# Token choice of layer 0 in a written order, with the context products of layer 1 beside it

## The chip, the cores and the metric

The kernel runs on one core of one Trainium2 chip. The metric is the device time of one execution in microseconds; the time of a kernel is the median of three runs. A profile is one further execution, recorded by the hardware profiler.

## The reference

Two layers work on x of 2 x 2048 tokens with 512 features, and on a context of 2 x 154 tokens. All of it is float32.

```python
x = x + L0_xattn(layernorm(x), ctx)                  # 16 heads
x = x + L0_ffn(layernorm(x))                         # below
x = x + L1_xattn(layernorm(x), ctx, Wq, bq, Wk, bk, Wv, bv)   # one head of 512
x = x + L1_ffn(layernorm(x))                         # top 2 of 8 experts, and a shared one

def L0_ffn(x):                                       # E = 8 experts, K = 1024
    scores = softmax(xf @ router_w + router_b)
    G, idx = top_k(scores.T, K)                      # each expert takes its 1024 best tokens
    toks = xf[idx]
    h1 = relu(toks @ w1 + b1); eo = h1 @ w2 + b2
    y[idx] += eo * G
```

So in layer 0 each expert chooses tokens: of 4096 scores the 1024 highest, ties to the lower token number. This choice is what the change rewrites, together with the products of layer 1's context (K, V and their like), which depend on inputs alone.

## The kernel before, in words

The kernel has four stages, one after the other. Attention of layer 0 ends with the scores of all tokens in `scores` (128 partitions, 8 experts x 32 token tiles) and with each normalized token and its scores in DRAM, 32 stores `xs<-row` (L403). Then comes the choice (L494 to L670). Then the experts of layer 0 run as 16 blocks of 512 tokens, with their products in a Strassen-like form of seven products of half blocks. Then follow attention and experts of layer 1.

The choice works in this way. Two transposes (`pt_s`, L573) bring the scores into the form of 8 experts x 16 runs of 256 tokens, one run a partition, and L574 copies them to `sco`. A search by bits then finds each expert's threshold, in 30 steps. In a step, DVE compares all scores with the threshold and counts a run (`cmp`, `cnt`, L591); PE sums the 16 counts of an expert with a matrix of ones, `same`, (`pc`, L579); DVE turns the sum into the next bit (`off`, L594) and the next threshold (`thr`, L595). Each of these waits for the one before it. After the search, L612 to L634 mark the chosen tokens (`sel`, `eq`), number them with two scans and two products with `tri` (`run`, `before`), transpose the numbers back (`pt_p`, L627) and split them into `hi` and `lo`.

From these the list of an expert's tokens is made: `list_head` (`ohhi`, `val`, L728 to L735), four times `list_part` (`ohlo`, L740) with `list_sum` (32 small products `ps_list`, L752), and `list_end` (`idx`, L764). With `idx`, POOL gathers token tiles from `xs` (`xg`, L773); `turn` transposes them (L112, `xgT`), and DVE makes sums of them (`xsum`, L791 to L794). POOL makes sums of the weights w1 (`sw`, L817). The products of a block (`prod`, L709) take turns with these. The first seven are p1, p6, p2, p7, p5, p3, p4; p1 needs `xgT` alone, p6 the second of `xsum` and the second of `sw`.

The context products are: `ps_k` (4 times 4 matmuls of 308 columns, L643), copied by ACT to `kpT`; `ps_kw` (the same with Wq, L650) to `kw`; `ps_bqk` (4, L658) to `bqk`; and `ps_v` (4 times 4 matmuls of 512 columns, L665), to which DVE adds the bias (`vp`, L668). `kw` and `vp` go to DRAM (L669, L670) and come back in layer 1. The profile counts each float32 matmul as two, since PE passes it twice; "x4" in a line is thus two matmuls.

What sets the order: attention and the experts stand in `tc.manual_schedule`, where the order of the code is the order on PE, DVE, ACT and POOL. The choice and the context products stand outside of it; there a scheduler orders each engine's instructions. It puts nine of the search's `pc` first, and then the products of `ps_k`, `ps_kw` and `ps_bqk` between the later ones; most of `ps_v` stands after the search. DMA issues on SP are always in the scheduler's order: w1q, ctxT, wk, wqT, wv, bq, bk, bv_bc, three more w1q, four w2q, kw_d, vp_d.

Memory: pools are stacked. `const` lasts for the whole kernel. `wm` holds the quarters of w1 and w2 (tags `w1` and `w2`, four buffers of 8 KB a partition each). `sr` and the PSUM pool `pr` hold all of the choice and of the context products, and are closed ahead of the experts, whose pools `sm` and `pm` take the same memory. A tile in such memory waits until the older tile's users, its DMAs among them, are done.

Of the kernel before, what the change touches and what calls it, by code (L numbers as in the profile page):

```python
# [20 lines left out]
P = 128  # L21
# [13 lines left out]
E = 8  # L35
# [20 lines left out]
def two_layers(ctx: ExitStack, tc: tile.TileContext, a, out):  # L56
# [34 lines left out]
    io_p = const.tile([P, 1], F32, name="io_p")  # L91

# [404 lines left out]
    with tc.tile_pool(name="wm", bufs=4) as wm:  # L497
# [9 lines left out]

        with (
            tc.tile_pool(name="sr", bufs=1) as sr,
            tc.tile_pool(name="pr", bufs=1, space=PSUM) as pr,  # L510
        ):

            ctxT = sr.tile([P, KC, B * TKV], F32, name="ctxT")
            nc.sync.dma_start(ctxT, a["ctxT"].rearrange("(k p) n -> p k n", p=P))
            wk = sr.tile([P, KC, D], F32, name="wk1")
            wv = sr.tile([P, KC, D], F32, name="wv1")
            wqT = sr.tile([P, KC, D], F32, name="wqT1")
            for w, n in ((wk, "Wk"), (wqT, "WqT"), (wv, "Wv")):
                nc.sync.dma_start(w, a[n].rearrange("(k p) n -> p k n", p=P))
# [8 lines left out]
            for q in range(4):  # L528
                load_w2(0, q)

            def iota(dst, pattern, mult):
                i = sr.tile(dst.shape, I32, name="iota_i")
                nc.gpsimd.iota(i, pattern=pattern, base=0, channel_multiplier=mult)
                nc.vector.tensor_copy(dst, i)

            iota(io128, [[1, P]], 0)
            iota(io8, [[1, CAP // P]], 0)
            iota(io_t, [[1, NT]], 0)
            iota(io_p, [[1, 1]], 1)

            same = sr.tile([P, E, NR], F32, name="same")
            tri = sr.tile([P, E, NR], F32, name="tri")
            nc.gpsimd.affine_select(
                same,
                ones.rearrange("p (e r) -> p e r", e=E),
                pattern=[[-NR, E], [0, NR]],
                compare_op=ALU.is_ge,
                fill=0.0,  # L550
                base=0,
                channel_multiplier=1,
            )
            nc.gpsimd.affine_select(
                same,
                same,
                pattern=[[NR, E], [0, NR]],
                compare_op=ALU.is_ge,
                fill=0.0,
                base=NR - 1,  # L560
                channel_multiplier=-1,
            )
            nc.gpsimd.affine_select(
                tri, same, pattern=[[NR, E], [1, NR]], compare_op=ALU.is_gt, fill=0.0, base=0, channel_multiplier=-1
            )
            same = same.rearrange("p e r -> p (e r)")
            tri = tri.rearrange("p e r -> p (e r)")
            half = RUN // P
            sco = sr.tile([P, half, P], F32, name="sco")
# [4 lines left out]
            nc.vector.tensor_copy(sco, pt)  # L574
            sco = sco.rearrange("p h n -> p (h n)")

            def per_expert(v, m, name):
                ps = pr.tile([P, 1], F32, tag="pc", name=name)
                nc.tensor.matmul(ps, m, v, start=True, stop=True)  # L579
                return ps  # L580
# [3 lines left out]
            thr = sr.tile([P, 1], I32, name="thr")  # L584
            nc.vector.memset(thr, 1 << 29)
            off = sr.tile([P, 1], I32, name="off")
            cmp = sr.tile([P, RUN], F32, name="cmp")
            cnt = sr.tile([P, 1], F32, name="cnt")
# [16 lines left out]
            nc.vector.memset(zero, 0.0)  # L605
# [6 lines left out]
            nc.vector.tensor_scalar(sel, sco, thrf, None, ALU.is_gt, ALU.add, accum_out=cnt)  # L612
            nc.vector.tensor_scalar(eq, sco, thrf, None, ALU.is_equal)
            pc = per_expert(cnt, same, "pc")
# [20 lines left out]


            kw = sr.tile([P, KC, B * TKV], F32, name="kw")
            vp = sr.tile([KV2, B, 2, D], F32, name="vp")
            kpT = sr.tile([P, KC, B * TKV], F32, name="kpT")
            for c in range(KC):  # L640
                ps = pr.tile([P, D], F32, tag="pre", name="ps_k1", bufs=2)
                for k in range(KC):
                    nc.tensor.matmul(  # L643
                        ps[:, : B * TKV], wk[:, k, ts(c, P)], ctxT[:, k, :], start=k == 0, stop=k == KC - 1
                    )
                nc.scalar.activation(kpT[:, c, :], ps[:, : B * TKV], AF.Identity, bias=bk[:, c : c + 1])
            for c in range(KC):
                ps = pr.tile([P, D], F32, tag="pre", name="ps_kw", bufs=2)
                for k in range(KC):
                    nc.tensor.matmul(  # L650
                        ps[:, : B * TKV], wqT[:, k, ts(c, P)], kpT[:, k, :], start=k == 0, stop=k == KC - 1
                    )
                nc.scalar.mul(kw[:, c, :], ps[:, : B * TKV], -scale1)
            bq_bc = sr.tile([P, KC, P], F32, name="bq_bc")
            nc.gpsimd.tensor_copy(bq_bc, bq.unsqueeze(2).to_broadcast([P, KC, P]))
            ps = pr.tile([P, D], F32, tag="pre", name="ps_bqk", bufs=2)
            for k in range(KC):
                nc.tensor.matmul(ps[:, : B * TKV], bq_bc[:, k, :], kpT[:, k, :], start=k == 0, stop=k == KC - 1)  # L658
            nc.scalar.mul(bqk, ps[:, : B * TKV], -scale1)
            for b in range(B):  # L660
                for j in range(2):
                    ps = pr.tile([P, D], F32, tag="pre", name="ps_v1", bufs=2)
                    n0 = b * TKV + j * KV2
                    for k in range(KC):
                        nc.tensor.matmul(  # L665
                            ps[:KV2, :], ctxT[:, k, n0 : n0 + KV2], wv[:, k, :], start=k == 0, stop=k == KC - 1
                        )
                    nc.vector.tensor_tensor(vp[:, b, j, :], ps[:KV2, :], bv_bc[:KV2, :], ALU.add)  # L668
            nc.sync.dma_start(kw_d, kw)  # L669
            nc.sync.dma_start(vp_d, vp)  # L670
# [16 lines left out]
        with (  # L687
# [36 lines left out]
            def list_head(e):  # L724
                shape = [P, NT, CAP // P]
                ohhi = sm.tile(shape, BF16, tag="ohhi", name="ohhi", bufs=1)
                val = sm.tile([P, NT, 2, CAP // P], BF16, tag="val", name="val", bufs=1)
                nc.vector.tensor_tensor(  # L728
                    ohhi,
                    hi[:, e, :].unsqueeze(2).to_broadcast(shape),  # L730
                    io8.unsqueeze(1).to_broadcast(shape),
                    ALU.is_equal,
                )
                nc.vector.tensor_tensor(val[:, :, 0, :], ohhi, io_t.unsqueeze(2).to_broadcast(shape), ALU.mult)
                nc.vector.tensor_scalar_mul(val[:, :, 1, :], ohhi, io_p)  # L735
                lst[e] = (val, pm.tile([P, 2, CAP // P], F32, tag="tr", name="ps_list"))

            def list_part(e, q):
                oh = sm.tile([P, LG, P], BF16, tag="ohlo", name="ohlo")
                nc.vector.tensor_tensor(  # L740
                    oh,
                    lo[:, e, q : q + LG].unsqueeze(2).to_broadcast([P, LG, P]),
                    io128.unsqueeze(1).to_broadcast([P, LG, P]),
                    ALU.is_equal,
                )
                lst[e, q] = oh
# [13 lines left out]
            def list_end(e):  # L760
                _, ps = lst.pop(e)
                part = sm.tile([P, CAP // P], F32, tag="part", name="part")
                nc.vector.tensor_copy(part, ps[:, 1, :])
                nc.vector.scalar_tensor_tensor(idx[:, e, :], ps[:, 0, :], float(P), part, ALU.mult, ALU.add)  # L764
# [4 lines left out]
            def gather(b, t):  # L769
                e, half = divmod(b, CAP // TB)  # L770
                col = half * TPB + t
                xg[b, t] = sm.tile([P, ROW], F32, tag="xg", name="xg", bufs=4)
# [7 lines left out]
            def turn(b, t):  # L780
                e = b // (CAP // TB)
                if t == 0:
                    xT[b] = sm.tile([P, KC, TB], F32, tag="xT", name="xgT", bufs=1)
                g = xg.pop((b, t))
                gates[b, t] = sm.tile([P, 1], F32, tag="gate", name="gate", bufs=12)
                nc.vector.tensor_copy(gates[b, t], g[:, D + e : D + e + 1])
                transpose_tile(g[:, 0:D], xT[b], t, pm, "tr")
# [12 lines left out]
            def sum_x(b):  # L800
                xsum[b] = sm.tile([P, 3, 2, HB], F32, tag="xsum", name="xsum", bufs=1)
# [10 lines left out]
            def sum_w1(b, q, part):  # L812
                a11, a12, a21, a22 = blocks_of_w1(b // (CAP // TB), q)
                for i in (0, 1) if part == 0 else (2, 3):
                    o = s1w[b, q, i] = sm.tile([P, 2, 2, P], F32, tag="sw", name="sw", bufs=6)
# [163 lines left out]

            list_head(0)  # L980
# [6 lines left out]
            sum_w1(0, 0, 0)  # L987
            sum_w1(0, 0, 1)
            sum_w1(0, 1, 0)
# [702 lines left out]
```

## Time and profile before

| what | us |
|---|---|
| median of three runs | 3005.03 (3000.24 to 3007.15) |
| the profiled execution | 3016.07 |
| its span | 3014.4 |
| PE busy in the span | 2778.1 (92%) |
| DVE, ACT, POOL busy | 1547.0, 880.1, 1216.7 |
| last scores of layer 0 written | 627.6 |
| search: first comparison to `sel` | 634.22 to 681.62 |
| `lo` written, list begun (`ohhi`), `idx` written | 689.94, 703.58, 710.12 |
| first gather, first product of a block (p1), p6 | 711.18, 719.90, 723.71 |

Times inside the profile are counted from the span's start. A line of a timeline has start, length, engine, line of the code, operation, tiles (out<-in), shapes, how many; in brackets stands how long the engine had been idle and what ended that. PE is the array, PEld its weight loads, SPq what SP issues. The granted clock is the share of full speed that PE was given in the stretch. A table of stretches gives the engines' busy time in each.

### The profile page before, as it was taken

The page shows a single profiled execution, that of the slowest core. Times are in us where ns is not written, and L with a number is a line of the kernel's source. Part 1 is how long each engine was busy: PE and PEld are TensorE (multiplying, and loading weights), DVE is VectorE, ACT ScalarE, POOL GpSimd, SP SyncE. Part 2 cuts the span into 40 slices and gives each one's busy share as a digit, 9 for nine tenths or more (in the row PEclk, how much of TensorE's full clock was granted, in tenths as well). Part 3 has the DMA queues.
Part 4 walks back from the last instruction along what each step waited for, and adds up shares of the span by engine and source line. Part 5 has one row for each costly group of instructions (what it writes and reads, how often), then busy time and mean ns, then how long its engine had stood idle before and what let it go on. Part 6 is the DMA issues. An engine that isn't in the chain of part 4 may idle for free. (4 is left out here: it accounts for less than half of the span.)

```text
span 3014.4 us, 38792 instructions
## 1 busy us (share of the span) xinstructions
PE 2778.1 (92%) x14262; PEld 2133.2 (71%) x14262; DVE 1547.0 (51%) x2933; ACT 880.1 (29%) x1854; POOL 1216.7 (40%) x986
## 2 busy tenths in 40 slices
PE   7889998867999999999999999999995888889995
PEld 4444554445888888888888888888885655567773
DVE  4677776544545435444454355443532555544355
ACT  2555554411122112212122112211220555432331
POOL 1445544403344424343334333432431555465552
PEclk9899999878999999999999999999998999899998
DMA  4011111161122231231222312312113642143387
GB/s 160 18 36 46 47 61 47 53 219 38 25 77 84 44 111 25 78 86 27 67 81 70 88 22 78 88 29 85 56 15 80 220 81 64 47 92 129 133 315 282
DMA packets 127083, 256.47 MB, mean 85 GB/s; under 512 B 16508, under 2 KB 22668, under 8 KB 126742
## 3 DMA queue, kind: packets, MB, share of 16 engines
q1 hardware_dynamic: 93232, 170.79, 16.9%
q0 software_dynamic: 29056, 74.81, 10.8%
q10 hardware_dynamic: 4608, 8.39, 0.7%
q8 instruction: 115, 1.88, 0.3%
q14 instruction: 72, 0.59, 0.1%
HBM read 176.09 MB, written 77.85 MB: 84 GB/s over the span
## 5 line engine op out<-in xcount | busy, mean ns | idle before, releaser
L831 ACT ACTIVATE H<-H,b_sb 128x256 f32<-128x256 f32 (+1 forms) x384 | 198.9, 571 | 563.0 <-DVE H L882 287.0
L928 POOL TENSOR_TENSOR eo<-eo,b_bc 128x512 f32<-128x512 f32 x64 | 96.4, 1506 | 647.4 <-DVE eo L974 585.4
L709 PE MATMUL prod<-w2q,H 128*128 128x256 f32 x1536 | 346.9, 379 | 0.0
L709 PEld LDWEIGHTS prod<-w2q,H 128*128 128x128 f32 x1536 | 289.5, 190 | 38.1
L312 POOL TENSOR_TENSOR pr<-pr,sm 128x616 f32<-128x616 f32 x128 | 155.2, 1213 | 275.5 <-DVE sm L311 249.7
L709 PE MATMUL prod<-xsum,sw 128*128 128x256 f32 x1024 | 245.4, 380 | 0.7 <-DVE xsum L792 0.7
L709 PE MATMUL prod<-xgT,w1q 128*128 128x256 f32 x1024 | 243.2, 380 | 0.0
L709 PE MATMUL prod<-xgT,sw 128*128 128x256 f32 x1024 | 243.1, 380 | 0.0
L709 PE MATMUL prod<-tw,hs 128*128 128x256 f32 x1024 | 234.5, 380 | 0.0
L817 POOL TENSOR_TENSOR sw<-w1q 128x512 f32<-128x512 f32 x128 | 189.6, 1481 | 84.3 <-PE prod L709 84.0
L709 PEld LDWEIGHTS prod<-xgT,w1q 128*128 128x128 f32 x1024 | 195.5, 191 | 26.8
L709 PEld LDWEIGHTS prod<-tw,hs 128*128 128x128 f32 x1024 | 192.8, 190 | 27.8 <-PE prod L709 2.5
L709 PEld LDWEIGHTS prod<-xsum,sw 128*128 128x128 f32 x1024 | 193.3, 190 | 26.7 <-POOL sw L817 1.0
L709 PEld LDWEIGHTS prod<-xgT,sw 128*128 128x128 f32 x1024 | 193.4, 190 | 25.7
L113 ACT COPY xgT<-pt 128x512 f32<-128x512 f32 x64 | 37.5, 585 | 431.7 <-PE pt L112 431.7
L900 POOL DMA_INDIRECT xacc<-eo,idx x64 | 100.6, 1572 | 153.0 <-DMA xacc<-eo,idx 92.1
L1513 PE MATMUL ph<-xgT,wc 128*128 128x128 f32 x1248 | 152.6, 275 | 7.4 <-DVE wc L1503 6.0
L289 DVE TENSOR_REDUCE mx<-sc 128x4 f32<-128x616 f32 x128 | 101.8, 795 | 105.5 <-PE sc L285 103.5
L1513 PEld LDWEIGHTS ph<-xgT,wc 128*128 128x128 f32 x1248 | 145.6, 192 | 9.0 <-issue 5.3
L1528 PE MATMUL po<-wall,h1r 128*128 x312 | 146.7, 593 | 1.7 <-issue 1.7
L1536 DVE TENSOR_TENSOR y<-po,wall 128x512 f32<-128x512 f32 x78 | 53.9, 691 | 144.1 <-PE po L1528 134.1
L1485 POOL DMA_INDIRECT xg<-xn,xrow x78 | 84.1, 1079 | 106.6 <-PE pt L1120 100.6
(296 smaller groups left out, 5156.9 us busy)
## 6 DMA issues: line engine op xcount, KB each, us to landing
w1q<-in_w SPq DMA_DIRECT2D x32, 1024.0 KB
w2q<-in_w SPq DMA_DIRECT2D x32, 1024.0 KB
y<-ys SPq DMA_DIRECT2D x40, 256.0 KB
xs<-row SPq DMA_DIRECT2D x32, 260.0 KB
x_sb<-in_x SPq DMA_DIRECT2D x32, 256.0 KB
x<-in_x SPq DMA_DIRECT2D x32, 256.0 KB
xacc<-x SPq DMA_DIRECT2D x32, 256.0 KB
x<-xacc SPq DMA_DIRECT2D x32, 256.0 KB
```

Of the source, the lines that this page charges most:

```text
L113: nc.scalar.copy(dstT[:, :, ts(t, P)], pt)
L289: nc.vector.tensor_reduce(mx, sc[:, :, 0:TKV], AX.X, ALU.min)
L312: nc.gpsimd.tensor_tensor(pr, pr, sm.to_broadcast([P, 4, TKV]), ALU.mult)
L709: nc.tensor.matmul(ps[:, g, :], w, m, start=i == 0, stop=i == len(terms) - 1)
L817: nc.gpsimd.tensor_tensor(o, l, m, ALU.add if i == 0 else ALU.subtract)
L831: nc.scalar.activation(dst, src, AF.Relu, bias=b1_sb[:, e, f : f + 1])
L900: nc.gpsimd.indirect_dma_start(out=xacc[:, :], out_offset=bass.IndirectOffsetOnAxis(ap=idx[:, e, col : col + 1], axis=0), in_=eo, in_offse ...
L928: nc.gpsimd.tensor_tensor(eo, eo, b2_bc, ALU.add)
L1485: nc.gpsimd.indirect_dma_start(out=xg[r], out_offset=None, in_=G_.xn[:, :], in_offset=bass.IndirectOffsetOnAxis(ap=G_.xrow[:, i : i + 1], ...
L1513: nc.tensor.matmul(ph[:, c, :], wc[:, k * HE + c * P : k * HE + (c + 1) * P], x_[:, k, :], start=k == 0, stop=k == KC - 1,)
L1528: nc.tensor.matmul(po_[r], h[:, c, :], wflat[:, bass.ds(at + (W2_AT + c * D), D)], start=c == 0, stop=c == HE // P - 1)
L1536: nc.vector.tensor_tensor(y, po_.pop(r), wflat[:, bass.ds(at + B2_AT, D)], ALU.add)
```

## The change

The stage of choice and context products now also stands in `manual_schedule`. Its pieces:

- The iota constants, `same`, `tri` and the tiles of the search (`sco`, `cmp`, `cnt`, `off`, `thr`) move to `const`, and the constants are made at the kernel's start.
- The context products become a generator, `ctx_part`. After each `pc` or `before` product, `per_expert` lets it put out one piece: two matmuls of 308 columns, or one of 512. What is left follows after the last use of the search.
- Wk, WqT, ctxT and Wv are loaded into the four buffers with the tag `w2`, in this order, ahead of w1; the four quarters of w2 come when these are free. In the order that the built program has on SP: Wk, WqT, ctxT, Wv, bq, bk, bv_bc, four w1q, two w2q, kw_d, one w2q, vp_d, one w2q.
- The bias of `vp` is added by POOL, after a copy by ACT, and not by DVE. `zero` is set by POOL.
- The list's tiles, gathered rows, `xgT`, `xsum`, `sw` and `gate` move to a pool `sl` and a PSUM pool `pl` of their own, opened before `sr` and `pr`; `sm` and `pm` keep the rest.
- `sum_w1` of the first block stands ahead of the list in the code. In the built program its six additions stand on POOL ahead of the four additions for `vp`, and the four gathers come behind those.
- `pc` after the search stands ahead of `eq` in the code, and `room` so comes ahead of the first scan on DVE.

```diff
+    def iota(dst, pattern, mult, name):
+        i = const.tile(dst.shape, I32, name=name)
+        nc.gpsimd.iota(i, pattern=pattern, base=0, channel_multiplier=mult)
+        nc.vector.tensor_copy(dst, i)
...
+    sco = const.tile([P, RUN], F32, name="sco")
+    cmp = const.tile([P, RUN], F32, name="cmp")
+    cnt = const.tile([P, 1], F32, name="cnt")
+    off = const.tile([P, 1], I32, name="off")
+    thr = const.tile([P, 1], I32, name="thr")
+    nc.vector.memset(thr, 1 << 29)
...
+        def load_ctx(n, cols):
+            t = wm.tile([P, 4, D], F32, tag="w2", name=n + "1")[:, :, 0:cols]
+            nc.sync.dma_start(t, a[n].rearrange("(k p) n -> p k n", p=P))
+            return t
+
+        sl = outer0.enter_context(tc.tile_pool(name="sl", bufs=2))
+        pl_ = outer0.enter_context(tc.tile_pool(name="pl", bufs=2, space=PSUM))
         with (
             tc.tile_pool(name="sr", bufs=1) as sr,
             tc.tile_pool(name="pr", bufs=1, space=PSUM) as pr,
+            tc.manual_schedule(engines={ET.PE, ET.DVE, ET.Activation, ET.Pool}),
         ):
-            ctxT = sr.tile([P, KC, B * TKV], F32, name="ctxT")
-            nc.sync.dma_start(ctxT, a["ctxT"].rearrange("(k p) n -> p k n", p=P))
...
+            wk = load_ctx("Wk", D)
+            wqT = load_ctx("WqT", D)
+            ctxT = load_ctx("ctxT", B * TKV)
+            wv = load_ctx("Wv", D)
...
             for q in range(4):
                 load_w1(0, q)
-            for q in range(4):
-                load_w2(0, q)
...
+            def ctx_part():
+                def sums(w, m, n):
+                    ps = pr.tile([P, D], F32, tag="pre", name="ps_c", bufs=2)
+                    for k in range(KC):
+                        nc.tensor.matmul(ps[: w(k).shape[1], 0:n], w(k), m(k), start=k == 0, stop=k == KC - 1)
+                        if k < KC - 1 and (k % 2 or n == D):
+                            yield ps
+                    yield ps
+
+                for c in range(KC):
+                    for ps in sums(lambda k: wk[:, k, ts(c, P)], lambda k: ctxT[:, k, :], B * TKV):
+                        yield
+                    nc.scalar.activation(kpT[:, c, :], ps[:, : B * TKV], AF.Identity, bias=bk[:, c : c + 1])
...
+                        for ps in sums(lambda k: ctxT[:, k, n0 : n0 + KV2], lambda k: wv[:, k, :], D):
+                            yield
+                        nc.scalar.copy(vp[:, b, j, :], ps[:KV2, :])
+                        nc.gpsimd.tensor_tensor(vp[:, b, j, :], vp[:, b, j, :], bv_bc[:KV2, :], ALU.add)
+                nc.sync.dma_start(vp_d, vp)
+
+            beside = ctx_part()
...
             def per_expert(v, m, name):
                 ps = pr.tile([P, 1], F32, tag="pc", name=name)
                 nc.tensor.matmul(ps, m, v, start=True, stop=True)
+                next(beside, None)
                 return ps
...
-            nc.vector.memset(zero, 0.0)
+            nc.gpsimd.memset(zero, 0.0)
...
+            pc = per_expert(cnt, same, "pc")
             nc.vector.tensor_scalar(eq, sco, thrf, None, ALU.is_equal)
-            pc = per_expert(cnt, same, "pc")
...
-                    nc.vector.tensor_tensor(vp[:, b, j, :], ps[:KV2, :], bv_bc[:KV2, :], ALU.add)
-            nc.sync.dma_start(kw_d, kw)
-            nc.sync.dma_start(vp_d, vp)
+            for _ in beside:
+                pass
+            for q in range(4):
+                load_w2(0, q)
...
-                ohhi = sm.tile(shape, BF16, tag="ohhi", name="ohhi", bufs=1)
-                val = sm.tile([P, NT, 2, CAP // P], BF16, tag="val", name="val", bufs=1)
+                ohhi = sl.tile(shape, BF16, tag="ohhi", name="ohhi", bufs=1)
+                val = sl.tile([P, NT, 2, CAP // P], BF16, tag="val", name="val", bufs=1)
...
+            sum_w1(0, 0, 0)
+            sum_w1(0, 0, 1)
+            sum_w1(0, 1, 0)
             list_head(0)
...
             for t in range(TPB):
                 gather(0, t)
-            sum_w1(0, 0, 0)
-            sum_w1(0, 0, 1)
-            sum_w1(0, 1, 0)
```

More of the change, by code (lines that the diff above doesn't have):

```diff
@@ L91, in two_layers @@
     io_p = const.tile([P, 1], F32, name="io_p")
+    def iota(dst, pattern, mult, name):
+        i = const.tile(dst.shape, I32, name=name)
+        nc.gpsimd.iota(i, pattern=pattern, base=0, channel_multiplier=mult)
+        nc.vector.tensor_copy(dst, i)
+    iota(io128, [[1, P]], 0, "io128_i")
+    iota(io8, [[1, CAP // P]], 0, "io8_i")
+    iota(io_t, [[1, NT]], 0, "io_t_i")
+    iota(io_p, [[1, 1]], 1, "io_p_i")
+    same = const.tile([P, E, NR], F32, name="same")
+    tri = const.tile([P, E, NR], F32, name="tri")
+    nc.gpsimd.affine_select(
+        same,
+        ones.rearrange("p (e r) -> p e r", e=E),
+        pattern=[[-NR, E], [0, NR]],
+        compare_op=ALU.is_ge,
+        fill=0.0,
+        base=0,
+        channel_multiplier=1,
+    )
+    nc.gpsimd.affine_select(
+        same,
+        same,
+        pattern=[[NR, E], [0, NR]],
+        compare_op=ALU.is_ge,
+        fill=0.0,
+        base=NR - 1,
+        channel_multiplier=-1,
+    )
+    nc.gpsimd.affine_select(
+        tri, same, pattern=[[NR, E], [1, NR]], compare_op=ALU.is_gt, fill=0.0, base=0, channel_multiplier=-1
+    )
+    same = same.rearrange("p e r -> p (e r)")
+    tri = tri.rearrange("p e r -> p (e r)")
+    half = RUN // P
+    sco = const.tile([P, RUN], F32, name="sco")
[4 more added lines that the diff above has]
+    nc.vector.memset(thr, 1 << 29)
     def layernorm(src, dst, small):
@@ L496, in two_layers @@
     vp_d = dram.tile([KV2, B, 2, D], F32, name="vp_d")
-    with tc.tile_pool(name="wm", bufs=4) as wm:
+    with ExitStack() as outer0:
+        wm = outer0.enter_context(tc.tile_pool(name="wm", bufs=4))
         w1s, w2s = {}, {}
@@ L510, in two_layers @@
             tc.tile_pool(name="pr", bufs=1, space=PSUM) as pr,
+            tc.manual_schedule(engines={ET.PE, ET.DVE, ET.Activation, ET.Pool}),
         ):
-            ctxT = sr.tile([P, KC, B * TKV], F32, name="ctxT")
-            nc.sync.dma_start(ctxT, a["ctxT"].rearrange("(k p) n -> p k n", p=P))
[L515 to L519, printed above, removed]
+            wk = load_ctx("Wk", D)
+            wqT = load_ctx("WqT", D)
+            ctxT = load_ctx("ctxT", B * TKV)
+            wv = load_ctx("Wv", D)
             bq = sr.tile([P, KC], F32, name="bq")
@@ L527, in two_layers @@
                 load_w1(0, q)
-            for q in range(4):
-                load_w2(0, q)
[L531 to L569, printed above, removed]
+            kpT = sr.tile([P, KC, B * TKV], F32, name="kpT")
+            kw = sr.tile([P, KC, B * TKV], F32, name="kw")
+            vp = sr.tile([KV2, B, 2, D], F32, name="vp")
@@ new lines, in two_layers @@
+            bq_bc = sr.tile([P, KC, P], F32, name="bq_bc")
+            nc.gpsimd.tensor_copy(bq_bc, bq.unsqueeze(2).to_broadcast([P, KC, P]))
+            def ctx_part():
[10 more added lines that the diff above has]
+                    nc.scalar.activation(kpT[:, c, :], ps[:, : B * TKV], AF.Identity, bias=bk[:, c : c + 1])
+                for c in range(KC):
+                    for ps in sums(lambda k: wqT[:, k, ts(c, P)], lambda k: kpT[:, k, :], B * TKV):
+                        yield
+                    nc.scalar.mul(kw[:, c, :], ps[:, : B * TKV], -scale1)
+                for ps in sums(lambda k: bq_bc[:, k, :], lambda k: kpT[:, k, :], B * TKV):
+                    yield
+                nc.scalar.mul(bqk, ps[:, : B * TKV], -scale1)
+                nc.sync.dma_start(kw_d, kw)
+                for b in range(B):
+                    for j in range(2):
+                        n0 = b * TKV + j * KV2
+                        for ps in sums(lambda k: ctxT[:, k, n0 : n0 + KV2], lambda k: wv[:, k, :], D):
+                            yield
+                        nc.scalar.copy(vp[:, b, j, :], ps[:KV2, :])
+                        nc.gpsimd.tensor_tensor(vp[:, b, j, :], vp[:, b, j, :], bv_bc[:KV2, :], ALU.add)
+                nc.sync.dma_start(vp_d, vp)
@@ L573, in two_layers @@
                 nc.tensor.transpose(pt[:, i, :], by_run[:, i, :], ident)
-            nc.vector.tensor_copy(sco, pt)
-            sco = sco.rearrange("p h n -> p (h n)")
+            nc.vector.tensor_copy(sco.rearrange("p (h n) -> p h n", h=half), pt)
             def per_expert(v, m, name):
@@ L579, in per_expert @@
                 nc.tensor.matmul(ps, m, v, start=True, stop=True)
+                next(beside, None)
                 return ps
[L584 to L588, printed above, removed]
             thrf = thr.bitcast(F32)
@@ L634, in two_layers @@
             nc.vector.tensor_copy(lo, pos)
[L637 to L667, printed above, removed]
-                    nc.vector.tensor_tensor(vp[:, b, j, :], ps[:KV2, :], bv_bc[:KV2, :], ALU.add)
-            nc.sync.dma_start(kw_d, kw)
-            nc.sync.dma_start(vp_d, vp)
+            for _ in beside:
+                pass
+            for q in range(4):
+                load_w2(0, q)
         HB = TB // 2
@@ L735, in list_head @@
                 nc.vector.tensor_scalar_mul(val[:, :, 1, :], ohhi, io_p)
-                lst[e] = (val, pm.tile([P, 2, CAP // P], F32, tag="tr", name="ps_list"))
+                lst[e] = (val, pl_.tile([P, 2, CAP // P], F32, tag="tr", name="ps_list"))
             def list_part(e, q):
-                oh = sm.tile([P, LG, P], BF16, tag="ohlo", name="ohlo")
+                oh = sl.tile([P, LG, P], BF16, tag="ohlo", name="ohlo")
                 nc.vector.tensor_tensor(
@@ L761, in list_end @@
                 _, ps = lst.pop(e)
-                part = sm.tile([P, CAP // P], F32, tag="part", name="part")
+                part = sl.tile([P, CAP // P], F32, tag="part", name="part")
                 nc.vector.tensor_copy(part, ps[:, 1, :])
@@ L771, in gather @@
                 col = half * TPB + t
-                xg[b, t] = sm.tile([P, ROW], F32, tag="xg", name="xg", bufs=4)
+                xg[b, t] = sl.tile([P, ROW], F32, tag="xg", name="xg", bufs=4)
                 nc.gpsimd.indirect_dma_start(
@@ L782, in turn @@
                 if t == 0:
-                    xT[b] = sm.tile([P, KC, TB], F32, tag="xT", name="xgT", bufs=1)
+                    xT[b] = sl.tile([P, KC, TB], F32, tag="xT", name="xgT", bufs=1)
                 g = xg.pop((b, t))
-                gates[b, t] = sm.tile([P, 1], F32, tag="gate", name="gate", bufs=12)
+                gates[b, t] = sl.tile([P, 1], F32, tag="gate", name="gate", bufs=12)
                 nc.vector.tensor_copy(gates[b, t], g[:, D + e : D + e + 1])
-                transpose_tile(g[:, 0:D], xT[b], t, pm, "tr")
+                transpose_tile(g[:, 0:D], xT[b], t, pl_, "tr")
             def combine(t_, b11, b12, b21, b22):
@@ L800, in sum_x @@
             def sum_x(b):
-                xsum[b] = sm.tile([P, 3, 2, HB], F32, tag="xsum", name="xsum", bufs=1)
+                xsum[b] = sl.tile([P, 3, 2, HB], F32, tag="xsum", name="xsum", bufs=1)
                 combine(xsum[b], *blocks_of_x(b))
@@ L814, in sum_w1 @@
                 for i in (0, 1) if part == 0 else (2, 3):
-                    o = s1w[b, q, i] = sm.tile([P, 2, 2, P], F32, tag="sw", name="sw", bufs=6)
+                    o = s1w[b, q, i] = sl.tile([P, 2, 2, P], F32, tag="sw", name="sw", bufs=6)
                     l, m = ((a21, a22), (s1w.get((b, q, 0)), a11), (a11, a21), (a12, s1w.get((b, q, 1))))[i]
```

## The prediction

> **What bounds the kernel now.** I first read the table of stretches, then the timeline of the stage that the diff touches (628 to 724 us from the span's start), then the waits, the DMA rates and the dependencies in the built programs. Everywhere else PE is the bound (1545 of 1558 us busy between 760 and 2318). Here it isn't. Columns: stretch, length, busy time of PE, PEld, DVE, ACT, POOL, granted clock, DMA share, GB/s.
>
> ```profile
> 628.00:634.20 6.20, 0.21 (x2) 0.02 (x1) 1.06 (x6) 0.00 (x0) 1.32 (x5) 0.68 0.93 312
> 634.20:648.00 13.80, 5.35 (x19) 4.70 (x20) 7.13 (x38) 0.00 (x0) 0.90 (x3) 0.50 1.06 384
> 648.00:654.20 6.20, 6.20 (x16) 4.16 (x17) 2.35 (x12) 0.52 (x1) 0.00 (x0) 0.50 1.04 387
> 668.00:681.60 13.60, 13.60 (x62) 9.26 (x61) 8.06 (x41) 2.23 (x5) 0.00 (x0) 1.00 0.01 1
> 690.00:703.50 13.50, 8.34 (x20) 2.66 (x18) 2.06 (x3) 0.00 (x0) 0.00 (x0) 0.94 0.14 47
> 703.50:711.20 7.70, 1.51 (x32) 1.17 (x32) 5.92 (x9) 0.00 (x0) 0.02 (x1) 0.50 0.19 68
> ```
>
> The stage is a chain on DVE. It stands still twice for memory that an older tile still holds, 4.52 us ahead of the search and 4.51 us ahead of the list; between lie 13.5 us in which only the v products run. In the timeline:
>
> ```profile
> 632.54 0.42 DVE L574 COPY sco<-pt_s 128x256 f32<-128x256 f32 x1 [4.52 <-DMA xs<-row]
> 649.31 2.40 PE L643 MATMUL ps_k<-ctxT,wk 128*128 128x308 f32 x4
> 651.50 0.42 PE L579 MATMUL pc<-cnt,same 128*128 128x1 f32 x2
> 670.02 0.37 PE L579 MATMUL pc<-cnt,same 128*128 128x1 f32 x2
> 670.25 1.28 PE L650 MATMUL ps_kw<-kpT,wqT 128*128 128x308 f32 x4
> 671.37 0.37 PE L579 MATMUL pc<-cnt,same 128*128 128x1 f32 x2
> 703.58 0.42 DVE L728 TENSOR_TENSOR ohhi<-hi,io 128x256 bf16<-128x256 bf16 x1 [4.51 <-DMA vp_d<-vp]
> ```
>
> A search step with two context products (four passes) beside it takes 1.35 us at full clock (670.02 to 671.37) and 2.48 at half clock (651.50 to 653.98, PE full); without products it takes 1.55 at half clock.
>
> **The change, part by part.**
>
> *Earlier start.* With sco, cmp, cnt, thr in constant memory, the copy no longer waits for the stores of xs: pt_s ends at 628.2, the first comparison can start at 628.8 instead of 634.22. That is 5.4 us, and I count it as lost. In the built order the first two context products stand between the first and second pc on PE, and they wait for Wk and ctxT. SP issues Wk where it issued w1q (629.72), then WqT, then ctxT. The DMA engines are full there:
>
> ```profile
> GB/s 223 391 362 230 293 360 397 388 382 395 387 385 393 385 391 379 354 349 393 395 395 391 377 389 385 391 391 383 383 385 391 391 385 379 387 391 170 0 0 0
> ```
>
> Each figure is 1 us from 628. Ahead of ctxT's end lie 1.06 MB of xs, 1.05 of Wk, 1.05 of WqT and 0.63 of ctxT, 3.79 MB: the sum of the row reaches that at 639.0. From the last bytes of xs (about 631.4) to the end of the wait for them passed 0.9 us, so ctxT is there at 639.9 (639 to 641). Late next is PE's queue: pc 2 stands behind the pair.
>
> *Search with products in each step.* PE idles 630 to 640, so it is at half clock. Pair one takes 2.2 us to the next pc: pc 2 at 642.1. The granted clock changes only on a grid of 3.41 us; all 22 rises in this trace follow a stretch with PE at least 0.95 busy, while two full stretches (from 647.3 and 2603.2) brought no rise yet. Half-clock steps fill PE, so the rise comes 3.4 to 6.8 us after 639.9, and up to 10.2 with such a miss. I take 645.1: 1.2 slow steps, 1.13 us extra each, 1.3 (0.8 to 3.4). 28 steps of 1.35 are 37.8; from pc 30 to sel 0.8. The search ends at 642.1 + 37.8 + 1.3 + 0.8 = 682.0, against 681.62 before: **+0.4**. The v steps carry two passes of 0.43, less than the four that 1.35 hides.
> The Trainium skill ("TensorE: Matmul & The Clock Gate", "What's actually happening") has one busy window of about 3.4 us suffice; the full stretch from 647.3 contradicts it as a certainty. By the rule the term would be at most 2.1.
>
> *POOL beside the DVE chain.* The built order puts the six sums sw (1.27 each, 7.7 us) ahead of the vp adds, so they run in the search when w1q lands (6.15 MB in the DMA row, with Wv and bv: 645.2, plus 0.9), about 646 to 656; before, POOL was idle. Such work stops DVE:
>
> ```profile
> 2416.43 0.19 DVE L1110 TENSOR_TENSOR oh<-act,gates 128x32 f32<-128x32 f32 x1
> 2416.77 1.27 POOL L1218 TENSOR_TENSOR x<-x,sb_bc 128x512 f32<-128x512 f32 x1 [3.08 <-ACT xn L1214]
> 2417.10 0.98 DVE L1113 TENSOR_TENSOR oh<-oh,fh_m 128x32 f32<-128x32 f32 x1
> 821.45 1.38 POOL L928 TENSOR_TENSOR eo<-eo,b_bc 128x512 f32<-128x512 f32 x1 [2.19 <-DVE eo L977]
> 821.73 1.38 DVE L734 TENSOR_TENSOR val<-ohhi,io_t 128x256 bf16<-128x256 bf16 x1
> ```
>
> The same small operation takes 0.19 alone and 0.98 when POOL is in a tensor_tensor; it ends when POOL does. DVE's reductions beside POOL don't stretch (L310 0.78 either way). In a step, the update of thr reads two tiles, so it can be caught; for cmp (L591, accumulating) no row shows it. First catch: half a POOL operation, 0.64; then POOL's 1.28 and the step's 1.35 run in step, some 0.13 each for five more: 1.3. The vp adds now on POOL: two in the search, 0.6 each, 1.2. **+2.5** (0 to 7.5, if cmp is caught too). The search ends at 684.5.
> The Trainium skill ("SBUF — State Buffer", "SBUF: two separate sides") speaks against this part: it calls the shared port pair an exclusive lock, held for the whole instruction, by GpSimd against a DVE operation with two SBUF inputs or in a 2-port mode. The rows agree for two inputs; no run here shows cmp beside POOL.
>
> *From search to list.* Before: sel at 681.62, lo written at 689.94, ohhi at 703.58: 21.96 us. After, ohhi waits for hi alone and ps_list has its own banks. sel to lo: 8.3 before; room now goes ahead of the scan (+0.4); pt_p no longer queues behind four v passes (-0.6); pos no longer waits for a vp add on DVE (-0.4): 7.7. The third vp add on POOL catches the scan (up to 1.15, taken whole): 8.9. **-13.1.** The v products finish behind pt_p, under the list; the last vp add falls on ohhi or val: L734 shows 1.38 against 0.43, **+1.0** (0 to 1.2). idx: 684.5 + 8.9 + 6.5 + 1.0 = 700.9, before 710.12.
>
> *Gather to products.* Unchanged in form. vp_d and the last two w2q loads move in front of the gathers on SP, 2.7 MB or 7 us after about 690, done by 699; gather 1 would issue at 702. The sums are done, so p6 no longer waits for xsum (1.67 and 1.75 beside POOL, 0.68 without): -0.7. Half clock lasted 2.5 us into the first product before; with a grid that falls anywhere, 1.7 us longer on average, at 45% loss: +0.8. Sum 0.
>
> *Costed at nothing.* The iota and selects at the start: POOL waits 8.16 us for ctxT there; DVE's four casts (0.85) delay xn by 0.5, while PE is kept by wk until 12.99. Without cover: 0.9. Loads of w2q late: first used over 20 us into the first block. ACT copies of vp (0.6 each): ACT is idle. The hand-over to layer 1: the built order shows the same waits.
>
> **Sum:** 0.4 + 2.5 - 13.1 + 1.0 + 0 = -9.2, say **-9**. On the profiled execution (3016.07, span 3014.4) 3007; I take it off the median of the runs, 3005.03: **2996**.
>
> **Rivals.**
> 1. *POOL doesn't catch the chain*: all port terms gone (2.5, 1.15, 1.0): -13.8, 2991. For: the 0.13 per step is my timing. Against: the L1113 rows.
> 2. *cmp is caught too*: each step then waits for a further POOL operation (1.28, and 0.3 for thr), over three steps 4.8, less the 1.3 counted, and 0.6 at each of two adds: -4.3, 3001.
> 3. *No wait for ctxT*: search from 628.8, 10 us more: -19, 2986. The byte count speaks against it.
> 4. *Slower: the clock stays at half through the search.* Place: pc 2 to 30. 18 steps of 2.48 and 12 of about 2.1 instead of 1.35 are some 27 us, net +18: 3023. It decides from eight slow steps (9/1.13) beyond those counted. Against: PE is full at half clock, and full stretches have always brought the rise within two.
> 5. *It doesn't do what it says*: the list still waits for vp_d; what is left is the longer search, 3008. The built waits speak against it.
>
> **Numbers.** Forecast 0.53, rival 1 0.16, 2 0.13, 3 0.04, 4 0.05, 5 0.04, others 0.05 (half of them slower). Range 2986 to 3004: it takes in rivals 1 to 3 and the spread of the runs (7 us). A measurement here tells 0.2%, 6 us: faster by more 0.72 (forecast mostly, 1, 3), within 0.20 (2, 5, the forecast's edge), slower 0.08 (4, others).
>
> **What would show it.** sco at about 628.4; PE idle until about 640 with ps_c ended by a DMA; steps of 1.35 once the clock is full; thr or cmp at over 0.16 or 0.48 between 646 and 656; ohhi within 0.2 us of lo; idx at about 701. The prediction is wrong if ps_c doesn't wait, if the clock stays at half, or if ohhi still shows a DMA.

## The result and the profile after

The changed kernel takes 2995.06 us (median of 14 runs, 2990.15 to 3000.33), the kernel before 3002.54 us (14 runs beside them). The ratio is 0.9969, with a 95% interval of 0.9962 to 0.9975: 7.5 to 11.4 us less, where 9 were predicted (9.3 by the ratio; the medians differ by 7.5). Run twice more, beside the kernel before on each occasion, the changed kernel gave 0.9959 (0.9946 to 0.9973) and 0.9976 (0.9966 to 0.9986).

The profiled execution of the changed kernel has a span of 2993.9 us, 20.5 less than the one of before. That difference is not the change's alone. In three executions of the changed kernel the last scores were through PE at 632.8, 633.1 and 627.1 us (before 628.2): the clock falls to half at other points of layer 0's attention, for 68 us in all up to the scores in the first two and for 58 us in the third and in before. From the last `prod` of layer 0 to the end it took 695.8, 694.5 and 693.7 us (before 709.1); but the code of that part is the same in all thirteen profiles of this document, and it takes 692.6 to 714.5 us in them, with 55 to 79 us at half clock; `best`, below, alone has 710.5 and 692.6. And the profiled execution of before, at 3016.07, was slower than all 14 timed runs. So I count from the end of the last scores' transposes (`pt_s`) to the sixth product of the first block (p6), beyond which the main part is the same: 1581.6 us from p6 to the last `prod` in both kernels.

| us from the end of `pt_s` | before | predicted | after | again | third |
|---|---|---|---|---|---|
| first comparison | 6.0 | 0.6 | 0.5 | 0.5 | 0.5 |
| first context product | 19.5 | 11.7 | 12.5 | 12.2 | 12.6 |
| `sel` (search done) | 53.4 | 56.3 | 56.3 | 55.2 | 57.0 |
| `ohhi` (list begun) | 75.4 | 65.2 | 64.6 | 64.0 | 66.3 |
| `idx` written | 81.9 | 72.7 | 72.1 | 71.6 | 73.9 |
| p6 | 95.5 | 86.3 | 83.7 | 84.9 | 86.4 |

The stage is 11.8, 10.6 and 9.1 us shorter. ("After", "again" and "third" are three profiles of the changed kernel; "predicted" is the prediction's time on the axis of before, less 628.2.) First the beginning of the search, in the timeline of the changed kernel:

```profile
632.81 0.42 DVE L622 COPY sco<-pt_s 128x256 f32<-128x256 f32 x1 [0.38 <-PE pt_s L621]
633.27 0.48 DVE L634 TENSOR_SCALAR_CACHE_REDUCE cmp<-sco,thr 128x256 f32<-128x256 f32 x1
635.47 0.68 SPq L556 DMA_DIRECT2D ctxT<-in_ctxT  x1
645.27 2.39 PE L590 MATMUL ps_c<-ctxT,Wk 128*128 128x308 f32 x4 [10.87 <-issue]
647.46 0.43 PE L626 MATMUL pc<-cnt,same 128*128 128x1 f32 x2
647.92 0.16 DVE L637 TENSOR_SCALAR off<-pc 128x1 int32<-128x1 f32 x1 [12.61 <-PE pc L626]
```

The copy of the scores waits for PE alone; the 4.52 us for memory are gone. But DVE then stands still for 12.61 us in step two: its `pc` is queued on PE behind the first context products, and these start at 645.27. The row gives "issue" as their releaser, which means that the profile saw nothing; the run `ctx_first` below shows that it is ctxT's landing. The stretches, with the columns that the prediction explains:

```profile
633.80:645.20 11.40, 0.58 (x2) 0.50 (x2) 0.81 (x4) 0.00 (x0) 0.00 (x0) 0.50 1.04 351
645.20:649.40 4.20, 4.13 (x9) 2.96 (x10) 0.81 (x4) 0.00 (x0) 0.61 (x1) 0.50 1.05 371
659.00:688.50 29.50, 29.02 (x111) 14.56 (x110) 17.52 (x88) 3.81 (x8) 2.78 (x3) 1.00 0.30 93
```

In the first, the engines are almost idle and the DMA engines are full; in the second PE is full at half clock; in the third the search runs with PE full at full clock. Now the places where an operation of DVE's chain is caught by POOL, that is, runs longer beside a POOL operation:

```profile
651.28 1.26 POOL L828 TENSOR_TENSOR sw<-w1q 128x512 f32<-128x512 f32 x1 [2.49 <-DMA w1q<-in_w]
651.54 1.02 DVE L638 SCALAR_TENSOR_TENSOR thr<-off,thr 128x1 int32<-128x1 int32 x1
652.59 0.48 DVE L634 TENSOR_SCALAR_CACHE_REDUCE cmp<-sco,thr 128x256 f32<-128x256 f32 x1
655.06 1.26 POOL L828 TENSOR_TENSOR sw<-w1q,sw 128x512 f32<-128x512 f32 x1
655.10 1.25 DVE L638 SCALAR_TENSOR_TENSOR thr<-off,thr 128x1 int32<-128x1 int32 x1
689.98 1.26 POOL L613 TENSOR_TENSOR vp<-vp,bv_bc 77x512 f32<-77x512 f32 x1 [3.89 <-ACT vp L612]
690.12 1.67 DVE L652 TENSOR_TENSOR_SCAN run<-eq,zero 128x256 f32<-128x256 f32 x1
```

An update of `thr` takes 0.16 us elsewhere, and the scan 0.69; here they end when POOL's operation does, or later. `cmp`, which reads one tile and accumulates, keeps its 0.48 us beside POOL. Then the list:

```profile
697.21 0.29 DVE L677 CAST lo<-pos 128x256 bf16<-128x256 int32 x1
697.41 0.42 DVE L739 TENSOR_TENSOR ohhi<-hi,io 128x256 bf16<-128x256 bf16 x1
697.53 1.42 POOL L613 TENSOR_TENSOR vp<-vp,bv_bc 77x512 f32<-77x512 f32 x1 [6.29 <-ACT vp L612]
697.87 1.37 DVE L745 TENSOR_TENSOR val<-ohhi,io_t 128x256 bf16<-128x256 bf16 x1
704.65 0.17 DVE L775 SCALAR_TENSOR_TENSOR idx<-ps_list,part 128x8 uint32<-128x8 f32 x1
710.47 0.15 DVE L797 COPY gate<-xg 128x1 f32<-128x1 f32 x1 [5.65 <-DMA xg<-xs,idx]
716.47 0.89 PE L720 MATMUL prod<-xsum,sw 128*128 128x256 f32 x3 [0.43 <-DVE xsum L803]
```

`ohhi` follows `lo` at once, with no DMA in its bracket. `val` is caught by the last addition to `vp` (1.37 against 0.43). DVE waits 5.65 us for the first gathered tile, against 4.59 before; from its gather's issue that tile takes 5.35 us (705.12 to 710.47), against 3.52 (711.18 to 714.70).

### The profile page after: what moved, and what is told of

It reads as the page before. It is cut to its first block, busy times and chain, and to the rows that moved or that the text cites. A ratio compares the mean times of both kernels' runs of the same rounds, so it can differ in the third digit from the quotient of the medians.

```text
span 2993.9 us, 38789 instructions
## 1 busy us (share of the span) xinstructions
PE 2769.2 (92%) x14262; PEld 2124.6 (71%) x14262; DVE 1556.2 (52%) x2928; ACT 882.8 (29%) x1858; POOL 1213.9 (41%) x991
## 3 DMA queue, kind: packets, MB, share of 16 engines
q0 software_dynamic: 29056, 74.81, 10.9%
## 5 line engine op out<-in xcount | busy, mean ns | idle before, releaser
L828 POOL TENSOR_TENSOR sw<-w1q,sw 128x512 f32<-128x512 f32 x64 | 90.9, 1420 | 89.1 <-PE prod L720 89.1
L230 PE MATMUL ps_q<-xnT,wq 128*128 128x512 f32 x256 | 126.5, 640 | 0.0
```

What stands on the lines that cost most here:

```text
L230: nc.tensor.matmul(ps, wq[:, k, ts(c, P)], xnT[blk][:, k, :], start=k == 0, stop=k == KC - 1)
L828: nc.gpsimd.tensor_tensor(o, l, m, ALU.add if i == 0 else ALU.subtract)
```

## The experiments

Of before, one profile exists, and of most runs one too: differences of a microsecond between two of them can be the clock's. Times of runs are compared through the ratio to the kernel before, measured beside them.

**The changed kernel again** (`after_again`, `after_third`), without an edit.

> The changed kernel once more, as the base for the runs beside it. Theory: 0.997 of before (2995 us); from the end of the last scores to the sixth product 84.5 us, as in its first profile (before 96.1), give or take 2 us for where the clock's 3.41 us grid falls; first comparison 1.3 us after the last scores, first context product 12 us after that, and not before ctxT has landed. The time of layer 0's attention should differ from the first profile's by some us without any change of code; were it the early constants that made the scores end 4.4 us later than in before, it would be 4.4 us late again.

> The changed kernel, as the base for the two runs beside it: 0.996 to 0.997 of before; 83.7 to 85 us from the end of the last scores to the sixth product.

Measured: 0.9959 and 0.9976, and the columns of the table above; p6 of the third, 86.4, lies beyond the 85 expected. The scores ended at 633.1 and 627.1 us; with the same early constants, two of the variants below began the first row maximum of the attention at 58.6 and 58.8 us (before 58.7, `after` 59.8), and `list_only`, which leaves the constants where they were, at 60.5. So no cost of the constants can be seen; one below about 1 us can't be excluded.

**The list back in the old memory** (`list_back`). `val`, `ohlo` and `part` move likewise; the list's PSUM tile stays in its own banks.

```diff
-                ohhi = sl.tile(shape, BF16, tag="ohhi", name="ohhi", bufs=1)
+                ohhi = sm.tile(shape, BF16, tag="ohhi", name="ohhi", bufs=1)
```

> Only ohhi, val, ohlo and part go back into memory that the search stage's tiles hold. Theory (the list waited for memory, not for data): ohhi waits again, until the store of vp_d has landed, which is issued 1.5 us after lo is there and takes some 4 us: ohhi 6 to 8 us later than lo, and the kernel at about 3002 us (1.000 of before); the other half of the 13.6 us that the list gained in the first profile stays, since the v products now end ahead of lo. Rival (the list came earlier only because the v products moved into the search): ohhi still follows lo at once, 2995 us.

Measured: 3001.4 us, 0.9988 (0.9980 to 0.9997). The timeline:

```profile
694.87 0.29 DVE L677 CAST lo<-pos 128x256 bf16<-128x256 int32 x1
696.48 0.38 SPq L614 DMA_DIRECT2D vp_d<-vp  x1
702.88 0.42 DVE L739 TENSOR_TENSOR ohhi<-hi,io 128x256 bf16<-128x256 bf16 x1 [7.73 <-DMA vp_d<-vp]
```

DVE waits 7.73 us for the store of `vp`, of which the list needs no byte. The rival falls. p6 comes at 91.2 against 83.7 to 86.4, and most of the gain is gone: without memory of its own for the list, the rest of the change is worth 0.1%.

**Only the list's memory** (`list_only`), put into the kernel before. `val`, `ohlo` and `part` move likewise; `ps_list` and the transposes of the gathered rows go to `pl_`.

```diff
+        tc.tile_pool(name="sl", bufs=2) as sl,
+        tc.tile_pool(name="pl", bufs=2, space=PSUM) as pl_,
...
-                ohhi = sm.tile(shape, BF16, tag="ohhi", name="ohhi", bufs=1)
+                ohhi = sl.tile(shape, BF16, tag="ohhi", name="ohhi", bufs=1)
```

> The kernel before, with own memory for the list and its transposes (SBUF and PSUM) and nothing else of the change. Times from the end of the last scores. Theory (the wait for memory is the price; the products' place is another): search unchanged (first comparison 6.0, sel 53.4), ohhi follows lo at 61.8 instead of 75.4, but two of four ohlo stand behind the last vp add on DVE, which waits for the last v product at 70.1: idx at 74 instead of 81.9, sixth product at 87.6 instead of 95.5, so -8 us: 2998 us against 3006 (0.9974). Rival 1 (own memory alone gives the whole 13.6): idx at 68.3, 2992 us. Rival 2 (nothing is won while the v products stand ahead): idx 81, 3005 us.

Measured: 0.9979 (0.9969 to 0.9988), so 3.6 to 9.3 us; `sel` at 52.4, `ohhi` at 60.6, `idx` at 72.9, p6 at 87.7, 1.3 to 4.0 us behind the whole change.

```profile
690.25 0.41 DVE L732 TENSOR_TENSOR ohhi<-hi,io 128x256 bf16<-128x256 bf16 x1
695.34 0.69 DVE L672 TENSOR_TENSOR vp<-ps_v,bv_bc 77x512 f32<-77x512 f32 x1 [1.16 <-PE ps_v L669]
698.78 0.69 DVE L672 TENSOR_TENSOR vp<-ps_v,bv_bc 77x512 f32<-77x512 f32 x1 [2.75 <-PE ps_v L669]
699.39 2.35 DVE L744 TENSOR_TENSOR ohlo<-lo,io 128x1024 bf16<-128x1024 bf16 x2
```

`ohhi` no longer waits, but the last two `ohlo` stand behind the bias of the last v product. So two pools give 7.8 us of the stage, as expected, and both rivals fall; the products inside the search and the rest of the change add 1.3 to 4.0, at the price of a longer search.

**ctxT loaded ahead of WqT** (`ctx_first`).

```diff
-            wqT = load_ctx("WqT", D)
+            wqT = wm.tile([P, 4, D], F32, tag="w2", name="WqT1")[:, :, 0:D]
             ctxT = load_ctx("ctxT", B * TKV)
+            nc.sync.dma_start(wqT, a["WqT"].rearrange("(k p) n -> p k n", p=P))
```

> WqT's load is issued behind ctxT's instead of ahead of it; nothing else. Theory (the first product waits for ctxT's bytes): 1.05 MB less ahead of it at 385 GB/s, so the first product, the second pc and the end of the search come 2.7 us earlier: about 2992.5 us (0.9965). Rival (it waits for Wk, or for the queue of loads as a whole): no change, 2995.

```profile
632.70 0.66 PE L622 MATMUL pt_s<-ident,scores 128*128 128x128 f32 x2 [1.76 <-DVE scores L441]
643.23 2.39 PE L591 MATMUL ps_c<-ctxT,Wk 128*128 128x308 f32 x4 [8.25 <-issue]
645.87 0.16 DVE L638 TENSOR_SCALAR off<-pc 128x1 int32<-128x1 f32 x1 [9.98 <-PE pc L627]
```

The first product comes 9.9 us after the scores instead of 12.2 to 12.6, and DVE's wait falls from 12.61 to 9.98: near the 2.7 us expected for the 1.05 MB that now come later. Only ctxT's place in the queue moved, so the stall is ctxT's landing. `sel` comes at 52.8 instead of 55.2 to 57.0. In the time it does not show: 0.9962 (0.9948 to 0.9976), against 0.9959 of the changed kernel beside it; 2.7 us are 0.0009, less than either interval.

**No products in the first seven steps** (`late_pieces`).

```diff
+                calls.append(name)
+                if len(calls) > 7:
+                    next(beside, None)
-                next(beside, None)
```

> The first seven search steps carry no context products; the rest of them run later. Theory (the search stands still 11 us because PE's queue holds a product that waits for ctxT): eight steps of 1.55 us at half clock fill the wait, the first product starts at the landing of ctxT as before, and seven steps of 1.35 us are saved: -9.5 us in the search, some 0.3 back since eight v products now run behind the search: about 2986 us (0.9943). Rival 1 (the products that are pushed out behind the search hold up the list): -3 us, 2992. Rival 2 (the clock rises later, as PE is less busy ahead of the products): four more slow steps, -5 us, 2990.

Measured: 2987.96 us, 0.9942 (0.9929 to 0.9955), better than the 0.9959 beside it by 5 us (3.9 by the medians), with intervals that overlap. `sel` comes at 47.3, 8 to 9.7 us earlier, as the theory has it; rival 2 doesn't show there, though the clock rose latest of all here, 6.6 us after the first product. But of that p6 shows only 4 to 6 (80.1). Two things give the rest back:

```profile
683.50 5.74 PE L590 MATMUL ps_c<-Wv,ctxT 128*77 128x512 f32 x13
689.08 0.55 PE L767 MATMUL ps_list<-val,ohlo 128*128 128x16 bf16 x16
692.27 0.38 SPq L551 DMA_DIRECT2D w2q<-in_w  x1
694.04 1.23 POOL L788 DMA_INDIRECT xg<-xs,idx  x1 [2.22 <-DVE idx L779]
700.49 0.15 DVE L801 COPY gate<-xg 128x1 f32<-128x1 f32 x1 [6.75 <-DMA xg<-xs,idx]
```

The products that were pushed out now stand on PE ahead of `ps_list`, and `lo` to `idx` takes 9.0 us instead of 7.3 to 7.4. And the last load of w2q, which waits for Wv's buffer, is issued 1.8 us ahead of the gathers: DVE waits 6.75 us for the first gathered tile, and the last comes 10.9 us after `idx` instead of 8.0 to 8.6. So rival 1 is right in part: the products cost the list some 1.6 us, and the gathers, with loads beside them on the DMA engines, take longer, which no theory had.

**The six sums behind the gathers again** (`sums_late`).

```diff
-            sum_w1(0, 0, 0)
-            sum_w1(0, 0, 1)
-            sum_w1(0, 1, 0)
             list_head(0)
...
                 gather(0, t)
+            sum_w1(0, 0, 0)
+            sum_w1(0, 0, 1)
+            sum_w1(0, 1, 0)
```

> The changed kernel with the six sums of w1 back behind the first gathers, as before. Theory (POOL's operations lock out DVE's update of thr): no update of thr over 0.2 us, so the search takes 1 to 2 us less from the first context product to sel (42.9 to 43.8 in the runs so far, then 42); but the sums meet the four xsum again, which take 1.1 to 1.75 instead of 0.69, and hold up the sixth product by 1 to 2 us: net 0 to -1, about the time of the changed kernel beside it (0.996 of before). Rival (the long thr are not POOL's): they stay, and the sums behind the gathers only cost, +1.5 us.

Measured: 0.9973 (0.9964 to 0.9982), like the changed kernel's. No update of `thr` is over 0.2 us; from the first context product to `sel` it takes 42.3 us, against 43.8, 43.0 and 44.4. These 0.8 to 2.1 us are paid again behind the gathers:

```profile
710.24 1.48 DVE L802 TENSOR_TENSOR xsum<-xgT 128x512 f32<-128x512 f32 x1 [1.38 <-ACT xgT L157]
711.13 1.73 POOL L828 TENSOR_TENSOR sw<-w1q 128x512 f32<-128x512 f32 x1
711.75 1.66 DVE L803 TENSOR_TENSOR xsum<-xgT,xsum 128x512 f32<-128x512 f32 x1
713.56 1.97 PE L720 MATMUL prod<-xsum,sw 128*128 128x256 f32 x8 [2.24 <-DVE xsum L803]
```

p6 waits 2.24 us for `xsum`, against 0.43, and follows p1 by 4.1 us, against 2.4 in the first profile of the changed kernel (both at full clock, but for the first 0.2 us there). So the sums cost 0.8 to 2.1 us in the search and, in this one profile, 1.7 us behind the gathers. p6 comes at 83.3, no later than in the changed kernel (83.7 to 86.4), where the clock was not always full at p1.

**Together** (`best`, `best_again`; `best_sums` with the sums behind the gathers). To `ctx_first` it adds the skip of the first five steps, and the last two loads of w2q by ACT behind the first `turn`.

```diff
+                if len(calls) > 5:
+                    next(beside, None)
...
-            for q in range(4):
+            for q in range(2):
                 load_w2(0, q)
...
             sum_x(0)
+            for q in (2, 3):
+                load_w2(0, q, nc.scalar)
```

> ctxT loaded ahead of WqT, no context products in the first five search steps, and the last two loads of w2q issued by ACT behind the first gathers' transposes. Times from the end of the last scores. Theory: first context product at 9.9, pc never waits for it for more than 1 us, sel at 46 (changed kernel 55.2 to 56.3), idx at 61.5 (71.6 to 72.1), the gathers no longer share the DMA engines with w2q: sixth product at 73.5 to 74.5 (83.7 to 84.9), so -10 us: 0.993 of before, 2984 to 2986 us. Rival 1 (the gathers are slow by themselves, not by w2q): sixth product 15 us after idx as in the run with late pieces, 76.5, -7 us. Rival 2 (w2q now comes too late): the first block's output products wait, and the main part gets longer than 1581.6 us.

> The same with the six sums of w1 behind the first gathers. Theory of the locked port: against the run without this, -1 us in the search (no update of thr over 0.2 us), +1 to +2 at the sixth product: the same time within 1 us. Rival (the sums cost nothing where they were): +1.5 us.

> The best version so far, beside the changed kernel: sixth product at 75.7 us after the last scores, as in its first profile, so 8 to 9 us less than the changed kernel, 0.993 to 0.995 of before. Rival (the 8 us of the stage are given back later, as its first run hints): the time of the changed kernel.

Measured: `best` 0.9946 (0.9933 to 0.9959) and, on another occasion, 0.9954 (0.9938 to 0.9969), both a little above what was expected, where the changed kernel beside it has 0.9976 (0.9966 to 0.9986): 2987.2 against 2992.8 us. `best_sums` 0.9959 (0.9946 to 0.9973), with `sel` at 44.9 and p6 at 77.1: 1 us won in the search and 0.4 to 1.4 lost at p6, so the place of the sums makes no difference that these runs can tell. In the stage of `best`, `sel` comes at 46.1 and 45.9 us, and p6 at 75.7 and 76.8, 7 to 11 less than with the change alone. The main part stays at 1581.6 us, so w2q comes in time, and the whole gain reaches the last `prod` of layer 0. The gain in time, 5.6 us by the medians, is below that. What follows the last `prod` is the same code and took 710.5 and 692.6 us in the two profiles of `best`, with 75 and 55 us at half clock: a difference of a few us in the time can't be told from that spread.

```profile
642.01 0.59 PE L629 MATMUL pc<-cnt,same 128*128 128x1 f32 x2 [0.96 <-DVE cmp L639]
642.66 2.39 PE L591 MATMUL ps_c<-ctxT,Wk 128*128 128x308 f32 x4
```

The stall is gone: the first product follows the sixth `pc`. The search is as expected; the rest is not. `ohlo` took 6.77 us for four instead of 4.62, so `idx` is at 63.0 instead of 61.5. With w2q out of the way the first gathered tile comes 3.9 us after `idx` (5.5 to 6.1 in the changed kernel), but the second comes 2.9 us after the first, and p1 10.3 us after `idx`, no better than in the changed kernel (9.2 to 9.9). The store of `vp` is issued 2.2 us ahead of the first gather there. It has landed by 698.45, since SP's next issue waits for it; that issue is two loads of 256 KB each (`b_bc`), which go out 0.4 us behind the second gather, at 698.01. In the first profile of the changed kernel they go out ahead of all gathers. Whether the store or these loads delay the second tile wasn't tried.

**The bias on PE** (`best_bias`): as `best`, with one more product in place of POOL's addition.

```diff
+                    if n == D:
+                        nc.tensor.matmul(ps[:KV2, :], ones[0:1, :KV2], bv_bc[0:1, :], start=True, stop=False)
+                        yield ps
...
-                        nc.gpsimd.tensor_tensor(vp[:, b, j, :], vp[:, b, j, :], bv_bc[:KV2, :], ALU.add)
```

> The same, but the bias of vp is added on PE as one more product with a row of ones, so POOL adds nothing to vp. Theory of the locked port: all four ohlo take 4.6 us together instead of 6.8, val 0.43 and the scan 0.69; the four more passes on PE (0.86 us each) fall behind the search, so that ps_list waits for PE and idx comes at 63 to 64 us, no better than the 63.0 of the run without. Rival (ohlo was slow for another reason, such as PE or the memory): ohlo 6.8 us again, idx at 66.

```profile
685.12 2.35 DVE L758 TENSOR_TENSOR ohlo<-lo,io 128x1024 bf16<-128x1024 bf16 x2
688.23 3.66 PE L594 MATMUL ps_c<-Wv,ctxT 128*77 128x512 f32 x8
692.11 2.36 DVE L758 TENSOR_TENSOR ohlo<-lo,io 128x1024 bf16<-128x1024 bf16 x2 [4.64 <-PE ps_list L770]
```

With POOL silent the four `ohlo` take 4.71 us, so POOL's additions were what made them slow, and the rival falls. But `idx` is at 66.0, not at 63 to 64. I had overlooked that `ohlo` has two buffers: the third waits until `ps_list` has used the first, and `ps_list` waits on PE for the ten products that are left. The time is 0.9939 (0.9925 to 0.9954), the lowest ratio of all; its p6, at 79.0, is later than that of `best`, so nothing in the stage explains that, and I take it as the same as `best`.

## Why the prediction was right

The forecast was -9; the three stages give -11.8, -10.6 and -9.1, and the time -9.3 (-7.5 to -11.4). The largest term, from search to list, and the loss of the early start were right in mechanism and size; that the smaller terms add up so closely is in part luck, as said below.

- **Earlier start, lost to ctxT.** Right: first comparison 0.5 us after the scores, first product at 12.2 to 12.6 us where 11.7 was forecast. `ctx_first` shows the cause, `late_pieces` and `best` what the wait cost: with steps in its place the search ends 8 to 11 us earlier. Rival 3 (no wait) was thus not in the change; it could be had.
- **Search with products.** Right: in the first profile the clock rose 4.1 us after the first product, and the steps took 1.35 us. Rival 4 (half clock throughout) never came near: in eleven profiles of the change and its variants the rise came 3.3 to 6.6 us after the first product.
- **POOL beside the search, +2.5.** The mechanism is right; that the sum came out (`sel` at 56.3, 55.2 and 57.0, forecast 56.3) is luck in its parts. `thr` lost 1.95 us to the six sums in the first profile (twice, 0.86 and 1.09), 1.0 and 2.1 in the others, where I had 1.3. The two additions to `vp`, at 1.2, caught nothing in the first profile. `cmp` was never caught, so rival 2 falls; `sums_late` shows the sums' part by itself. The prediction says that the lock it quotes speaks against this part; the rows of `thr`, the scan and `val` show such a blocking, so it speaks for the part, and only against `cmp`.
- **From search to list, -13.1.** Measured -13.6, -13.2 and -12.6. `list_back` has `ohhi` 16.1 us after `sel` (8.3 in the first profile, 22.0 before): 7.8 of the 13.6 hang on memory there, and 5.8 remain, since the v products end earlier. In `list_only`, own memory alone brings `ohhi` to 8.2, but the list then waits for the v products. The scan was caught, as assumed (+0.98).
- **List, +1.0.** Measured +0.9, +1.0, +1.0, though in the second profile `ohlo` was caught and not `val`.
- **Gather to p6, 0.** Here lies the difference: -1.9, -0.3 and -1.1. `xsum` took 0.69 and p6's wait fell to 0.43, as said. I had w2q done by 699 us; it was issued at 696.9 and 699.4 and shared the DMA engines with the gathers. Yet the last tile came 8.0 to 8.6 us after `idx`, against 8.8: the four gathers are issued 1.25 us apart anyway, and the first now goes out 0.3 us after `idx`, where it was 1.1 before, which the prediction had not counted. The clock makes most of the spread: it was full 0.2 us after p1's start in the first profile, 3.4 and 2.3 us after it in the others, and 2.5 before.
- Rivals 1 and 5 are excluded by the caught operations and by `ohhi`.

What stays open: whether the constants at the start cost some tenths, why the second gather is late in `best`, and whether layer 1, behind the last `prod`, takes back any of the 7 to 11 us that `best` gains in the stage; its spread of 22 us between profiles hides it.

## What to carry to other kernels

When an engine waits on a store whose data it doesn't need, ask which pool its output tile shares: two pools of its own brought most of this change's gain. A product that is put beside a chain of short steps on the same engine must have its operands there when the first one is due; place the pieces by the landing time of their loads, and look at what the postponed ones then stand in front of. An operation moved to POOL to relieve DVE is not free where DVE's chain reads two tiles: it stretches that chain by up to its own length at each meeting, here by some 1 to 2 us in all, in the search or behind the gathers.

## What the hardware showed that I had not expected

The blocking goes both ways. POOL's addition to `vp`, 1.26 us alone, took 2.36 and 2.27 us in `best` beside `ohlo` (bf16, two tiles read); of the four `ohlo` two then took about 2.2 us, worked out from 6.77 for four and 1.16 for one alone. With POOL silent none did. And of six sums of 1.27 us that follow each other almost without a gap for 7.6 us, a chain that reads two tiles once in each step was caught by only one or two. A reading that fits the rows, but was not tested: the first catch shifts its steps against POOL's operations, so that the next updates end near the end of one (`thr` at 653.74 for 0.16 us, as a sum that began at 652.62 ended).
